# Depthwise taps as diagonal matmuls in 16 tiles of the array, the projection in row tiles, and one planner for all images

## The chip, the cores and the metric

One core of a Trainium2 chip runs the kernel in one launch. The metric is the device time of that launch in microseconds. Before the change the median of three runs is 9529.6 us (9521.79 to 9544.45).

## The reference, cut to what matters

The input is x, 64 images of 96 channels of 56x56 pixels in float32. Each image passes three parts, one after the other; C is 96, the middle width is 192, `bn` is a batch norm with fixed numbers.

```
out = silu(bn(expand_w @ x))                     # 1x1, 96 -> 192
out = channel_shuffle(shift_groups(out), 4)      # four groups moved by one pixel
dw  = bn(depthwise3x3(out)); idb = bn(out * id_w)
out = silu(bn(dw + idb))
se  = sigmoid(W2 @ relu(W1 @ mean_pixels(out)))  # grouped, 192 -> 24 -> 192
t   = silu(bn(proj_w @ (out * se)) + x)          # 192 -> 96
t   = t + bn(w2 @ real(ifft(relu(fft(relu(bn(w1 @ layernorm(t)))) * (r + i) + b))))
t   = t + ffn_fp8(layernorm(t))                  # 96 -> 384 -> 96, quantised
```

The Fourier transform runs over the 3136 pixels of an image for each of 192 channels.

## The kernel before, in words

Channels lie on partitions. The 96 channels of x and t stand in 112 partitions with a gap of 16 in the middle (`CP`, `GAP`), and one partition of the gap carries ones or a shift row. x has a border of one pixel (58x58), so that a shift is a window into it. x and t have two buffers each, by the image's parity (L104, L105); `load_x` (L112) fills an x buffer with two DMAs on SyncE's queue.

[...] the pool `psa` holds two tiles of two banks for the mixing, `psb` four tiles of one bank for all else.

An image goes through these functions, each a generator that yields after a step, so that steps of several images can be interleaved:

- `expand_a` (7 steps) and `expand_b` (5 steps): matmuls of 32 output columns, four side by side in the array (L297, L312), then a silu on ScalarE into `e_a` (128 channels, 58x58) or `e_b` (64 channels, the image's two halves stacked to 128 partitions, 30x58).
- `depthwise` (L329): three calls of nine steps, for the upper and lower half of `e_a` and for `e_b`. Each step is one VectorE instruction over 128x1568 elements (L341 for the first tap, L343 for the other eight), accumulating in `d_buf`. `mid_silu` (L346) applies bias and silu and sums the pixels, in three ScalarE instructions an image (L352).
- `excitation` (L357): the two small layers on the pixel sums, tanh in place of sigmoid, and the projection weights scaled by the gate (`pw`).
- `project` (L385): eight steps of seven rows, each three matmuls of 392 columns into one bank: an identity that brings x in (L395), the first 128 channels (L396) and the other 64 (L397). A silu writes t transposed (L400). After the last step it issues `load_x(b + 2)`.
- `deviations` (L406): the layer norm's factors. Per 448 columns one matmul centres t (L417), ScalarE squares (L419), four matmuls with one column take the mean (L426), VectorE adds epsilon (L427) and GpSimd raises to the power -0.5 (L428). `spread` puts the factors where the mixing needs them (L434, L441).
- `mixing` (L458): the Fourier part, in six stages that I call by the names of their plan: W1 (L468), F1 (L490), F2 (L518, L524, with ScalarE and VectorE steps L539 to L543 and `mirrored`), W2 (L555, L567), I1 (L590) and I2 (L608, added to t at L618).
- `ffn` (L628): 20 steps of layer norm and transposition (L639, L650, L656, L665), then 52 steps of the two fp8 layers (L674, L676, L684, L690, L692) and the store (L700, L702).

The order of all engines' work is written by a planner in the program (`merge`, L736). `PLAN` gives each stage of the mixing a length and each other function a first and a last due time, in the planner's own units counted from the start of one image's mixing. `merge` runs `mixing(b)` and after each of its steps all steps of the others that are due and whose needs are met; what is left is run when the mixing has ended, so nothing crosses from one image's mixing into the next. Beside `mixing(b)` run `ffn(b - 1)`, the last tap block, excitation, projection and deviations of image b + 1, and expand and the first two tap blocks of image b + 2. Images 0 and 1 are begun before the first mixing, one function after another. [...]

## Time and profile before

| what | value |
|---|---|
| median of three runs | 9529.6 us |
| the profiled execution, own time | 9484.53 us |
| its span | 9482.8 us |
| mean granted TensorE clock | 0.898 of full speed |
| instructions | 263604 |
| HBM read, written | 82.62 MB, 77.07 MB |
| one image's period in the middle (first W1 matmul to the next, median) | 146.7 us |
| first W1 matmul of image 0 | 172.7 us |
| end of the last image's mixing to the end of the span | about 51 us |

A row of the page's groups gives the source line, engine, operation and tiles, the shapes, the count, busy time in us, the mean of one in ns, and how long the engine was idle just before such instructions, with what ended that wait. An f32 matmul leaves two records, so counts of PE are twice the matmuls where the type is f32. Records of PE overlap: the time between two starts says more than the length of one. "PEclk" or "granted clock" is the share of full speed that the throttle gave TensorE.

### The profile page before, as it was taken

How to read it: one execution, taken by the hardware profiler on the slowest of the kernel's cores; microseconds unless marked ns; L12 is line 12 of the kernel's file. 1: busy time of each engine (PE TensorE's matmuls, PEld its weight loads, DVE VectorE, ACT ScalarE, POOL GpSimd, SP SyncE). 2: the span in 40 equal slices, each digit the busy share in tenths (PEclk: the TensorE clock that was granted, in tenths of full speed). 3: DMA queues.
4: the chain of work that ended last, by engine and by line, in shares of the span. 5: the costliest groups of instructions: out<-in, count | busy, mean ns of one | idle time of the engine just before them, and what ended most of it. 6: DMA issues, size and time to landing. Idle time of an engine off the chain costs nothing.

```text
span 9482.8 us, 263604 instructions
## 1 busy us (share of the span) xinstructions
PE 8133.7 (86%) x118530; PEld 6030.7 (64%) x118530; DVE 6389.5 (67%) x9034; ACT 4790.4 (51%) x9099; POOL 2240.6 (24%) x1360
## 2 busy tenths in 40 slices
PE   5888888888888888888888888888888888888887
PEld 3666666666666666666666666666666666666666
DVE  6667666666666766676666766666666666676764
ACT  2455454454554545545545545455455454554545
POOL 0222222222222222222222222222222222222221
PEclk8988999898888999999989989889998898888988
DMA  2111111111101111111111111111110111111100
GB/s 40 17 22 16 19 21 16 20 17 17 22 15 19 17 19 21 17 18 21 17 17 22 16 19 18 17 21 17 17 22 14 20 17 17 22 16 19 18 13 15
DMA packets 411399, 177.45 MB, mean 19 GB/s; under 512 B 366323, under 2 KB 409707, under 8 KB 410011
## 3 DMA queue, kind: packets, MB, share of 16 engines
q1 hardware_dynamic: 408508, 155.59, 13.0%
q8 instruction: 930, 15.24, 0.7%
q10 hardware_dynamic: 1264, 3.48, 0.1%
q0 software_dynamic: 496, 1.50, 0.1%
q14 instruction: 201, 1.64, 0.1%
HBM read 82.62 MB, written 77.07 MB: 17 GB/s over the span
## 4 chain that ended last, share of the span: by engine, by line
PE 67%; DVE 13%; ACT 9%; issue 6%; POOL 5%; DMA 0%; POOLq 0%; ACTq 0%; DVEq 0%
PE ps_f L490 8%; PE ps_i L608 7%; PE ps_c L417 5%; PE ps_i L590 5%; POOL rs L650 5%; PE ps_v L426 4%; PE ps_w L468 4%; PE ps_pj L395 4%; PE ps_w L555 4%; PE ps_pj L396 4%; PE ps_pj L397 3%; DVE d L343 3%; PE ps_f L524 3%; ACT h L684 3%; DVE buf_h L475 3%
## 5 line engine op out<-in xcount | busy, mean ns | idle before, releaser
L343 DVE SCALAR_TENSOR_TENSOR d<-e_a,taps,d 128x1568 f32<-128x1568 f32 x1024 | 1892.0, 1848 | 14.3
L428 POOL TENSOR_TENSOR rs<-v,mhalf 112x4 f32<-112x4 f32 x448 | 1060.1, 2373 | 2650.7 <-DVE v L427 2589.6
L700 POOL TENSOR_TENSOR o<-t,o 112x448 f32<-112x448 f32 x448 | 587.6, 1312 | 2921.7 <-DVE o L698 2921.7
L650 POOL TENSOR_TENSOR rs<-v,mhalf 112x4 f32<-112x4 f32 x448 | 582.8, 1301 | 1637.1 <-DVE v L649 1637.1
L343 DVE SCALAR_TENSOR_TENSOR d<-e_b,taps,d 128x1568 f32<-128x1568 f32 x512 | 943.4, 1843 | 0.5
L427 DVE TENSOR_SCALAR v<-ps_v 112x4 f32<-112x4 f32 x448 | 72.0, 161 | 1281.0 <-PE ps_v L426 1270.3
L490 PEld LDWEIGHTS ps_f<-f_tab,buf_h 128*64 128x64 f32 x24576 | 747.3, 138 | 163.5 <-DVE buf_h L475 57.2
L490 PE MATMUL ps_f<-f_tab,buf_h 128*64 128x58 f32 x24576 | 797.8, 223 | 40.0 <-DVE buf_h L475 40.0
L676 ACT CAST y<-ps_h 128x448 f16<-128x448 f32 x1344 | 723.9, 539 | 148.8 <-PE ps_h L674 130.2
L684 ACT CAST h<-y 128x448 fp8e5<-128x448 f16 x1344 | 770.4, 573 | 0.3 <-DVE y L681 0.3
L681 DVE TENSOR_SCALAR y<-y,qb 128x448 f16<-128x448 f16 x1344 | 649.1, 487 | 154.6 <-ACT y L676 135.4
L590 PE MATMUL ps_i<-inv_tab,buf_g 112*32 112x56 f32 x24576 | 482.4, 253 | 285.7 <-issue 284.8
L468 PE MATMUL ps_w<-w1c,t 112*64 112x96 f32 x14336 | 708.0, 250 | 0.0
L468 PEld LDWEIGHTS ps_w<-w1c,t 112*64 112x64 f32 x14336 | 611.6, 137 | 139.3 <-issue 117.0
L426 PEld LDWEIGHTS ps_v<-mean_m,sq 96*112 96x112 f32 x3584 | 516.2, 213 | 281.4 <-issue 257.2
L608 PE MATMUL ps_i<-r_tab,buf_h 64*64 64x56 f32 x14336 | 676.1, 276 | 1.0 <-ACT buf_h L597 1.0
L590 PEld LDWEIGHTS ps_i<-inv_tab,buf_g 112*32 112x32 f32 x24576 | 439.1, 139 | 339.8 <-issue 293.0
L608 PEld LDWEIGHTS ps_i<-r_tab,buf_h 64*64 64x64 f32 x14336 | 647.9, 189 | 5.0 <-ACT buf_h L597 1.1
L475 DVE SCALAR_TENSOR_TENSOR buf_h<-ps_w,rs_full 128x768 f32<-128x768 f32 (+1 forms) x512 | 437.3, 854 | 254.8 <-PE ps_w L468 245.8
L690 PE MATMUL ps_o<-h,q 128*112 128x448 fp8e5 x1344 | 421.3, 393 | 213.1 <-ACT h L684 213.0
L597 ACT COPY buf_h<-ps_i 128x896 f32<-128x896 f32 x192 | 174.0, 906 | 787.8 <-PE ps_i L590 787.8
L417 PE MATMUL ps_c<-t,center 112*96 112x448 f32 x896 | 553.2, 706 | 11.6 <-issue 10.9
(159 smaller groups left out, 14740.5 us busy)
## 6 DMA issues: line engine op xcount, KB each, us to landing
x<-in_x SPq DMA_DIRECT2D x128, 588.0 KB, 8.3
out_dram<-o SPq DMA_DIRECT2D x896, 84.0 KB, 1.9
l_tab<-in_tab_l ACTq DMA_DIRECT2D x1, 1624.0 KB
r_tab<-in_tab_r ACTq DMA_DIRECT2D x1, 1568.0 KB
t<-dev_t SPq DMA_DIRECT2D x64, 7.0 KB, 1.8
t<-dev_t SPq DMA_DIRECT2D x64, 5.2 KB
ex_row_p<-in_expand_row POOLq DMA_DIRECT2D x1, 336.0 KB, 4.2
s_p<-in_bn POOLq DMA_DIRECT2D x1, 288.0 KB, 4.0
```

The costliest lines, as they stand in the source:

```text
L343: nc.vector.scalar_tensor_tensor(dst, win, w, dst, ALU.mult, ALU.add)
L417: nc.tensor.matmul(cen, lhsT=center, rhs=t[:, g * 4 * CP : (g + 1) * 4 * CP], start=True, stop=True)
L426: nc.tensor.matmul(var[:, k : k + 1], lhsT=sq[:, k, :], rhs=mean_m, start=True, stop=True)
L428: nc.gpsimd.tensor_tensor(rs[:, js], v[:, js], mhalf[0:CP, 0:4], ALU.pow)
L468: nc.tensor.matmul(ps[hc * 64 : hc * 64 + 64, k, 0:C], lhsT=t[:, n0 : n0 + 64], rhs=w1c[:, hc * C : hc * C + C], start=True, stop=True,)
L475: nc.vector.scalar_tensor_tensor(h_v[:, :, d * NJ + j0 : d * NJ + j0 + n], ps[:, 0:n, 0:C].rearrange("p b c -> p c b"), 0.0, rs_full[:, d, ...
L490: nc.tensor.matmul(ps[r * 64 : r * 64 + 64, k, 0 : 2 * NK], lhsT=buf_h[:, n0 : n0 + 64], rhs=f_tab[:, r, :], start=True, stop=True,)
L590: nc.tensor.matmul(ps[p0 : p0 + 32, k, 0:HW], lhsT=u_v[:, oh * 48 + o, :], rhs=inv_tab[:, r, :], start=True, stop=True,)
L608: nc.tensor.matmul(ps[pr, bk, k, 0:HW], lhsT=buf_h[pr, n2 * 48 : n2 * 48 + 64], rhs=r_tab[pr, n2, :], start=True, stop=True,)
L650: nc.gpsimd.tensor_tensor(rs, v, mhalf[0:CP, 0:4], ALU.pow)
L676: nc.scalar.copy(y16, ps)
L684: nc.scalar.copy(held[i // 3][:, i % 3, :], held.pop(("y", i)), saturate=False)
```

## The change

- The nine taps become matmuls on TensorE. At the start a table `diag` is made of 32x32 diagonal blocks, one for each tap and each group of 32 channels. A depthwise call takes all four tiles of `psb`; for each tap it issues 16 matmuls of 7x56 columns, from four groups of channels (row tiles of the array) into four places of seven rows (column tiles). So a PSUM tile holds one channel group with its 28 rows spread over the partitions. Four ScalarE instructions then add the bias, apply silu and sum. `mid_silu` is gone. `d_buf` has the new layout, half, group, seven rows.
- Excitation follows that layout: 12 matmuls for the first layer, 24 for the second, one add and one tanh; the 0.5 of the sigmoid is folded into the projection weights.
- `project` works in two halves. Each issues 24 matmuls with 32 contraction rows in four row tiles, into four banks, and VectorE adds x in PSUM before the silu; the identity matmul is gone.
- `deviations` centres with four matmuls of 96 columns for each 448 pixels, as `ffn` does, and VectorE sums the squares, in place of the matmuls of one column.
- x has one buffer; `project(b)` ends with `load_x(b + 1)`.
- In `ffn` the second layer and the result come a step later.
- `merge` is replaced by `schedule`: every function of every image has a due time on one axis (image b is shifted by b times 116 units) and needs that reach across images, so a step can run beside any image's mixing. "hold" keeps all other planned functions out until the same function's next step, "part" keeps those that take all four banks out. The due times are new.

The core of the diff:

```
+NG = MID // 32
...
-    "mixing": (22.3, 18.0, 30.7, 18.0, 12.0, 23.2),
-    "ffn": (0.0, 63.5),
-    "expand_a": (1.2, 20.0),
-    "depthwise_2": (8.4, 36.3),
-    "silu_2": (37.3, 38.6),
-    "excitation": (42.0, 44.0),
-    "expand_b": (51.7, 59.7),
-    "project": (60.0, 86.0),
-    "depthwise_0": (80.6, 95.9),
-    "silu_0": (114.5, 118.3),
-    "depthwise_1": (96.1, 115.9),
-    "deviations": (87.0, 110.4),
-    "silu_1": (115.9, 118.2),
+    "mixing": (18.0, 18.0, 30.0, 18.0, 12.0, 20.0),
+    "ffn": (120.1, 178.7),
+    "expand_a": (-108.4, -87.5),
+    "expand_b": (-138.3, -112.4),
+    "depthwise_0": (-98.8, -98.7),
+    "depthwise_1": (-97.0, -92.0),
+    "depthwise_2": (-78.0, -74.3),
+    "excitation": (-74.6, -59.1),
+    "project": (-60.0, -40.0),
+    "deviations": (-60.8, -16.8),
...
-    x_buf = [const.tile([CP, PAD, PAD], F32, name=f"x_{i}") for i in range(2)]
+    xi = const.tile([CP, PAD, PAD], F32, name="x")
     t_buf = [const.tile([CP, NPIX + 8], F32, name=f"t_{i}") for i in range(2)]
-    for i in range(2):
-        nc.vector.memset(x_buf[i], 0.0)
-        nc.sync.dma_start(out=x_buf[i][GAP : GAP + 1].rearrange("p a b -> p (a b)"), in_=tab_ones)
+    nc.vector.memset(xi, 0.0)
+    nc.sync.dma_start(out=xi[GAP : GAP + 1].rearrange("p a b -> p (a b)"), in_=tab_ones)
...
+    eyes = load(tab_eyes, [128, 32], "eyes")
+    diag = const.tile([128, 2, 9, 32], F32, name="diag")
+    for h in range(2):
+        nc.vector.tensor_tensor(
+            diag[:, h],
+            eyes.unsqueeze(1).to_broadcast([128, 9, 32]),
+            taps[:, h, :].unsqueeze(2).to_broadcast([128, 9, 32]),
+            ALU.mult,
+        )
...
+    nc.vector.tensor_scalar(s[:, 0], s[:, 0], 0.5, None, ALU.mult)
+    for g in range(NG):
+        nc.vector.tensor_tensor(pj_w[:, g, :], pj_w[:, g, :], s[:, 0], ALU.mult)
...
-    d_buf = const.tile([128, 3 * HH, HW], F32, name="d")
-    def depthwise(b, i):
+    d_buf = const.tile([128, 2, NG, PJ, HW], F32, name="d")
+    def depthwise(b, i, cvs):
         if b >= NB:
             return
...
+        if b not in cvs:
+            cvs[b] = small.tile([128, 2, NG], F32, tag="sums", name="sums")
+        sums = cvs[b]
+        e, h, base = ((e_a, 0, 0), (e_a, 0, HH), (e_b, 1, 0))[i]
+        pss = [psb.tile([128, PJ, HW], F32, tag="psb", name="ps_d") for _ in range(4)]
+        for tap in range(9):
             dy, dx = divmod(tap, 3)
...
+            for j in range(4):
+                r0 = base + j * PJ + dy
+                for r in range(4):
+                    pr = slice(r * 32, r * 32 + 32)
+                    nc.tensor.matmul(
+                        pss[r][j * 32 : j * 32 + 32],
+                        lhsT=diag[pr, h, tap, :],
+                        rhs=e[pr, r0 : r0 + PJ, dx : dx + HW],
+                        start=tap == 0,
+                        stop=tap == 8,
+                    )
+            if tap % 3 == 2:
+                yield "hold"
+        for r in range(4):
+            s, g = (i, r) if i < 2 else (r // 2, 4 + r % 2)
+            nc.scalar.activation(
+                d_buf[:, s, g], pss[r], AF.Silu, bias=mid_b[:, g : g + 1], accum_out=sums[:, s, g : g + 1]
+            )
         yield
     def excitation(b, cvs):
             return
         sums = cvs[b]
         ps = psb.tile([128, 8], F32, tag="psb", name="ps_se")
-        for i in range(3):
+        for i in range(2 * NG):
+            s, g = divmod(i, NG)
             nc.tensor.matmul(
-                ps[0:24, 0:1], lhsT=rd_w[:, i // 2, :], rhs=sums[:, i : i + 1], start=i == 0, stop=i == 2
+                ps[0:24, 0:1], lhsT=rd_w[:, g, :], rhs=sums[:, s, g : g + 1], start=i == 0, stop=i == 2 * NG - 1
             )
...
+        ps = psb.tile([128, NG], F32, tag="psb", name="ps_se2")
+        gate = small.tile([128, NG], F32, tag="gate", name="gate")
+        for g in range(NG):
+            for j in range(4):
+                nc.tensor.matmul(ps[j * 32 : j * 32 + 32, g : g + 1], lhsT=ep_w[:, g, :], rhs=red, start=True, stop=True)
+        nc.vector.tensor_tensor(gate, ps, ep_b, ALU.add)
         yield
...
+        nc.scalar.activation(gate, gate, AF.Tanh, scale=0.5)
         yield
...
+        pw = small.tile([128, NG, CP], F32, tag="pw", name="pw", bufs=1)
+        nc.vector.scalar_tensor_tensor(
+            pw, gate.unsqueeze(2).to_broadcast([128, NG, CP]), 1.0, pj_w, ALU.add, ALU.mult
+        )
         cvs[b] = pw
         yield
     def project(b, cvs):
         if b >= NB:
             return
         pw = cvs.pop(b)
-        xi = x_buf[b % 2]
         tv = t_buf[b % 2][:, 0:NPIX].rearrange("p (b a) -> p b a", a=HW)
...
+        for s in range(2):
+            pss = [psb.tile([CP, PJ, HW], F32, tag="psb", name="ps_pj") for _ in range(4)]
+            for g in range(NG):
+                for j in range(4):
+                    pr = slice(j * 32, j * 32 + 32)
+                    nc.tensor.matmul(
+                        pss[j], lhsT=pw[pr, g, :], rhs=d_buf[pr, s, g], start=g == 0, stop=g == NG - 1
+                    )
+                if g == 2:
+                    yield "hold"
+            yield "hold"
+            for j in range(5):
+                if j < 4:
+                    r0 = s * HH + j * PJ
+                    nc.vector.tensor_tensor(
+                        pss[j], pss[j], xi[:, r0 + 1 : r0 + 1 + PJ, 1 : HW + 1], ALU.add
+                    )
+                if j:
+                    r0 = s * HH + (j - 1) * PJ
+                    nc.scalar.activation(
+                        tv[:, :, r0 : r0 + PJ], pss[j - 1].rearrange("p a b -> p b a"), AF.Silu, bias=pj_sh
+                    )
+                yield None if j == 4 else "hold"
+        load_x(b + 1)
...
...
+            cen = psb.tile([CP, 4, 128], F32, tag="psb", name="ps_c")
+            for k in range(4):
+                n0 = (g * 4 + k) * CP
+                nc.tensor.matmul(cen[:, k, 0:C], lhsT=t[:, n0 : n0 + CP], rhs=center, start=True, stop=True)
+            sqs[g] = work.tile([CP, 4, C], F32, tag="sq2", name="sq")
+            nc.scalar.activation(sqs[g], cen[:, :, 0:C], AF.Square)
         def variances(g):
-            sq = sqs.pop(g)
             js = slice(g * 4, g * 4 + 4)
...
+            nc.vector.tensor_reduce(v[:, js], sqs.pop(g), AX.X, ALU.add)
+            nc.vector.tensor_scalar(v[:, js], v[:, js], 1.0 / C, 1e-5, ALU.mult, ALU.add)
             nc.gpsimd.tensor_tensor(rs[:, js], v[:, js], mhalf[0:CP, 0:4], ALU.pow)
...
-            if m == 0:
-                held[j] = work.tile([128, 3, CH], F8, tag="h8", name="h8")
...
         def quantise(i):
+            if i % 3 == 0:
+                held[i // 3] = work.tile([128, 3, CH], F8, tag="h8", name="h8")
             nc.scalar.copy(held[i // 3][:, i % 3, :], held.pop(("y", i)), saturate=False)
...
-            yield
+            yield "part" if g <= ng else None
             if 2 <= g < ng + 2:
                 turn(g - 2)
-            yield
+            yield "part" if g <= ng else None
         n = 3 * NCH
-        for i in range(n + 5):
+        for i in range(n + 7):
             if i < n:
                 first(i)
             if 1 <= i <= n:
             yield
             if 2 <= i <= n + 1:
                 quantise(i - 2)
-            j, m = divmod(i - 5, 3)
-            if i >= 5 and m == 0 and j < NCH:
+            j, m = divmod(i - 6, 3)
+            if i >= 6 and m == 0 and j < NCH:
                 second(j)
-            if i >= 6 and m == 1 and j < NCH:
+            if i >= 6 and m == 2 and j < NCH:
...
+    SIDES = {
+        "ffn": (76, (("mixing", 0, None),)),
+        "expand_a": (7, (("project", 1, None),)),
+        "expand_b": (5, (("project", 1, None),)),
+        "depthwise_0": (4, (("expand_a", 0, 4),)),
+        "depthwise_1": (4, (("expand_a", 0, None),)),
+        "depthwise_2": (4, (("expand_b", 0, None),)),
+        "excitation": (4, (("depthwise_0", 0, None), ("depthwise_1", 0, None), ("depthwise_2", 0, None))),
+        "project": (14, (("excitation", 0, None), ("ffn", 2, None))),
+        "deviations": (10, (("project", 0, None), ("mixing", 1, 8))),
+    }
+    HOLD = ("depthwise_0", "depthwise_1", "depthwise_2", "project")
+    def schedule():
...
+        def one(until):
+            ready = [
+                (when, key)
+                for key, when in due.items()
+                if when < until
+                and (holder == [key] or not holder and not (part and key[0] in HOLD))
+                and met(SIDES[key[0]][1], key[1])
+            ]
+            if not ready:
+                return False
+            when, key = min(ready)
+            lo, hi = PLAN[key[0]]
+            step = next(sides[key], "end")
+            holder[:] = [key] if step == "hold" else []
+            part.discard(key)
+            if step == "part":
+                part.add(key)
+            if step == "end":
+                ended.add(key)
+                del due[key]
+            else:
+                done[key] = done.get(key, 0) + 1
+                due[key] = when + (hi - lo) / SIDES[key[0]][0]
+            return True
+        for b in range(NB):
+            while one(at):
+                pass
+            while ("deviations", b) not in ended:
+                one(1e9)
+            for w in mixing(b):
+                at += w
+                done["mixing", b] = done.get(("mixing", b), 0) + 1
+                while one(at):
+                    pass
+            ended.add(("mixing", b))
+        while one(1e9):
+            pass
...
```

## The prediction

> **What bounds the kernel now.** I read the page's engine shares, then the chain of waits, then the stretches of one image, then PE's own timeline. The shares say TensorE (PE) is the fullest engine and DVE second:
>
> ```profile
> PE 8133.7 (86%) x118530; PEld 6030.7 (64%) x118530; DVE 6389.5 (67%) x9034; ACT 4790.4 (51%) x9099; POOL 2240.6 (24%) x1360
> PE 67%; DVE 13%; ACT 9%; issue 6%; POOL 5%; DMA 0%; POOLq 0%; ACTq 0%; DVEq 0%
> L343 DVE SCALAR_TENSOR_TENSOR d<-e_a,taps,d 128x1568 f32<-128x1568 f32 x1024 | 1892.0, 1848 | 14.3
> L428 POOL TENSOR_TENSOR rs<-v,mhalf 112x4 f32<-112x4 f32 x448 | 1060.1, 2373 | 2650.7 <-DVE v L427 2589.6 <-DVE dev L432 59.4
> ```
>
> The reader should see that the taps (L343) are the biggest DVE item, but DVE is only 13% of the chain: the change moves work from the second engine to the first. Image after image repeats every 146.6 us. Cutting one such period where each mixing stage's first matmul starts (W1, F1, F2, W2, I1, I2) gives the table I work from. Columns: window, length, busy us and instructions of PE, PE weight load, DVE, ACT, POOL; granted PE clock, DMA share, GB/s.
>
> ```profile
> 4656.00:4686.70 30.70, 26.64 (x369) 18.57 (x367) 22.55 (x38) 13.92 (x27) 9.18 (x7) 1.00 0.00 1
> 4686.70:4704.40 17.70, 16.59 (x404) 13.45 (x404) 14.82 (x18) 14.84 (x32) 2.61 (x2) 1.00 0.09 24
> 4704.40:4740.60 36.20, 31.12 (x253) 19.63 (x254) 23.44 (x47) 29.64 (x57) 6.57 (x5) 0.95 0.09 25
> 4740.60:4759.40 18.80, 18.80 (x147) 13.66 (x147) 13.48 (x13) 7.39 (x12) 0.00 (x0) 1.00 0.18 20
> 4759.40:4783.40 24.00, 18.53 (x437) 14.69 (x436) 8.60 (x9) 5.95 (x9) 9.65 (x4) 0.72 0.51 38
> 4783.40:4802.60 19.20, 15.57 (x255) 14.24 (x254) 16.40 (x18) 2.98 (x7) 7.19 (x3) 0.65 0.01 2
> sum 146.60, PE 127.25 PEld 94.23 DVE 99.29 ACT 74.73 POOL 35.20; mean PE 21.21 PEld 15.71 DVE 16.55 ACT 12.45 POOL 5.87
> ```
>
> PE is idle 146.6 - 127.25 = 19.4 us per image. The last two rows show a second loss: the granted clock is 0.72 and 0.65. In us at full clock that is 24.0 x 0.28 + 19.2 x 0.35 + 36.2 x 0.05 = 15.2 us. So the period is about 112 us of PE work at full clock, 19 idle, 15 clock. What starts the slow clock is in PE's timeline of I1:
>
> ```profile
> 4763.43 0.86 PE L426 MATMUL ps_v<-mean_m,sq 96*112 96x1 f32 x8
> 4764.21 1.47 PE L590 MATMUL ps_i<-inv_tab,buf_g 112*32 112x56 f32 x101
> 4771.16 0.96 PE L590 MATMUL ps_i<-inv_tab,buf_g 112*32 112x56 f32 x27 [5.47 <-issue]
> 4772.05 1.81 PE L417 MATMUL ps_c<-t,center 112*96 112x448 f32 x2
> ```
>
> PE stops 5.47 us for nothing the profile names, inside a run of equal matmuls; afterwards ps_c takes 1.81 us instead of 0.97. In 4 us windows DMA moves 98 to 105 GB/s from 4756 to 4768, which is load_x (issued 4755.5); my reading is that PE's instructions queue behind it.
>
> [...] The trace has four column tiles only: 8 matmuls of L312 (16 records) start to next start in 1.46 us, where one untiled 392-column f32 matmul takes 0.66 (L395, start to start), so 8 x 0.66 / 1.46 = 3.6 times. [...] the same 112x4 pow takes 2373 ns at L428, beside taps, and 1301 at L650.
>
> **The change, part by part** (PE us per image at full clock).
> - Taps to PE: DVE loses 2835 us of L343 (both shapes) and 198 of L341, so 3033 / 64 = 47 us per image. PE gains 3 x 144 f32 matmuls of 392 columns. If all 16 tiles run together, a tap costs one 0.66: 3 x (9 x 0.66 + 0.4) = 19.0. Bounds: 17.8 (no tail)[...]. I take 19.0, since four tiles got 3.6 here.
> - Projection: out go 24 matmuls x 0.66 = 15.8. In come 48 of K=32 in four row tiles, 12 rounds x 0.66 = 7.9; I take 8.5 (bounds 7.9 and, at no gain, 15.8). The identity matmul becomes 8 DVE adds of 392 from PSUM, about 0.62 each as L618: 5 us of DVE. Four of them are queued ahead of F2's last pair of DVE steps, whose result W2's last group needs only 6 us later, so I cost that wait at nothing; without W2's first three groups it would be 2.5.
> - Squares: ps_c goes from 7 x 0.83 to four small matmuls like ps_n (8 records, 0.95): +0.9. ps_v goes, 7 x 0.69 = -4.8; in its place 7 DVE reductions of 0.54 (L648's row).
> - Excitation: 10 PE records become 72. L363 has 6 in 0.31 us, so 72 cost some 3.7, less 0.9 before: +2.5 (bounds 1 and 8, if they cost L372's 0.15 each).
> - Sum: 112 + 19.0 - 7.3 + 0.9 - 4.8 + 2.5 = 122.3. **PE work grows by 10 us per image.** ACT: three silus of 1.61 + 0.20 become twelve of about 0.55 + 0.20, +3.5 us; the squares' ACT work is as before.
> - One x buffer: load_x(b+1) is issued after project(b) instead of a period earlier. Two DMAs on SP's queue, behind the last projection add; dev_t rows and out_dram stores queue behind them briefly. It needs about 12 us. Until expand_b (first user) PE has W2's last group 1.8, six ps_c steps 5.7, I1 5.2 and one more ps_c, 13.7 us: hidden, by a little. Without that cover expand_b would wait up to 12.
> - Depthwise and projection take all four psb banks. Behind a finished block the next psb user waits for its first silu, some 1 us, five times; mixing's matmuls (psa) cover some of it. While PE runs a block of 6.3 us, ACT has nothing but its backlog.
> - The planner: working the due times through for a middle image puts expand_a and depthwise_0 in W1, depthwise_1 in F1, depthwise_2, excitation and half the projection in F2, the other half and six of the squares in W2, expand_b in I1 and I2. The first part of ffn stays in W1.
>
> **By stage** (before, then after). W1 30.7: PE 10.5 (W1 itself) + 8.7 (ps_n, ps_x) + 0.3 + 1.4 (expand_b's end) + 3.6 (four expand_a) + 6.3 = 30.8, with idle 2.5 instead of 4.1, because pow no longer waits for taps: 33.3. F1 17.7: 12.1 + 3.4 (ffn) + 2.7 + 6.3 = 24.5, idle as now: 25.5. F2 36.2: PE 27 but ACT 13.7 (F2) + 16.9 (ffn) + 3 + 2 = 35.6, already 29.6 there now, so ACT sets it: 37.5. W2 18.8: 9.2 + 4.2 + 5.7, plus a bank wait: 20.3. I1 and I2 together 43.2: PE 5.2 + 7.1 + 5.9 (four expand_b) + 2 = 20.2; ps_v and the 3.2 us wait for dev (DVE behind taps) are gone; the fetch stall, later against I1 than now, I put at 3.5 (0 to 5.5), other idle 3, clock loss 6.3 (0 to 12; now 13.4): 33. The sum is 149.6, **+3.0 per image**. Over 63 periods +189. The opening gets shorter: the first W1 starts at 172.7 us now, behind 47 us of image 0's taps and 31 of image 1's on DVE; with PE doing 19 I take 45 off. 189 - 45 = +144 on the profiled 9484.5 (span 9482.8), so 9629; the median of the runs, 9529.6, is 45 above that execution, and I carry the difference: **9675**.
>
> **Rivals.** (1) *The clock comes back*, and the change is faster. If load_x no longer starves I1, and denser work in I1 and I2 keeps the clock up, these stages take 20.2 + 3 = 23.2 and the period 139.8: 63 x -6.8 - 45 gives 9057; with the stall kept and half the clock loss, 144.6 and 9360. It decides when I1 and I2 fall below 30 us. For it: ps_v, the dev wait and 47 us of DVE go, and they stand in these very stages. Against: load_x still falls right ahead of I1, and PE was busy and slow at once. (2) *Sixteen tiles overlap poorly*[...] For it: the trace has no 16-tile case, and bank waits add to it. Against: 3.6 of 4. (3) *It cancels*: I1 and I2 at 30, no difference.
>
> **Numbers.** Mine 0.45, (1) 0.32, (2) 0.18, (3) 0.05. All of mine and (2) lie on the slow side, so slower 0.63, faster 0.32, same 0.05, within 0.2%, about what a measurement can tell. Mine alone spans 9550 to 9880 (clock loss and stall). The range 9190 to 10,090 leaves out the lower third of (1) and the upper half of (2).
>
> **What would show it.** PE busy at full clock near 122 us a period; 144 tap matmuls in 5.9 to 6.4 us (over 8: rival 2); projection's 24 in about 4.2; F1 near 25; POOL's pow near 1.0 us. Wrong if the clock of I1 and I2 is above 0.85, if no "issue" gap stands in I1, or if PE waits for psb banks beyond 6 us per image.

## The result and the profile after

The changed kernel takes 9693.5 us (median of four runs, 9687.0 to 9705.0), beside 9525.7 us for the kernel before on the same chip. The ratio is 1.0175, with a 95% interval of 1.0156 to 1.0193. **The change makes the kernel 1.75% slower.** The profiled execution is the one of 9686.95 us, with a span of 9685.1 us; the mean granted clock rises from 0.898 to 0.966.

Read the page in the same order as before: engine shares, chain, then the groups that the change added. In a group's row the two numbers behind the bar are busy us and mean ns of one record (records overlap: the 36,864 of the first ps_d row, 497 ns each, make 1098.0 us).

```profile
PE 8671.6 (90%) x179970; PEld 6371.6 (66%) x179970; DVE 3865.7 (40%) x8218; ACT 4814.9 (50%) x10190; POOL 1488.0 (15%) x1360
...
PE 69%; ACT 13%; DVE 12%; issue 4%; POOL 1%; DMA 0%; POOLq 0%; ACTq 0%; SPq 0%; DVEq 0%
...
L355 PE MATMUL ps_d<-e_a,diag 32*32 32x392 f32 x36864 | 1098.0, 497 | 28.1 <-ACT y L700 27.9
...
L412 PE MATMUL ps_pj<-d,pw 32*112 32x392 f32 x6144 | 740.2, 557 | 33.6 <-ACT t L426 28.4
...
L454 POOL TENSOR_TENSOR rs<-v,mhalf 112x4 f32<-112x4 f32 x448 | 442.3, 1010 | 1228.7 <-DVE v L453 1228.7
...
L355 PE MATMUL ps_d<-e_b,diag 32*32 32x392 f32 x18432 | 569.4, 497 | 13.5 <-ACT y L700 11.6
```

DVE has lost 2524 us and PE has gained 538, although PE now runs nearly always at full clock (0.966 on the mean). The taps are 1098.0 + 569.4 = 1667 us, 26.1 us per image; three blocks, so 8.7 us a block where I had said 6.3. The projection is 740.2 / 64 = 11.6 us per image, not 8.5. GpSimd's pow (L454) takes 1.01 us, as I said it would when no taps run beside it; beside taps it took 2.37 (L428 of the kernel before).

These are the stages W1, F1, F2, W2, I1, I2 of one image in the middle. The columns are those of the windows before: window, length, busy us and instructions of PE, PE weight load, DVE, ACT, POOL; then clock, DMA share, GB/s.

```profile
4788.60:4821.90 33.30, 30.81 (x644) 23.47 (x632) 15.84 (x31) 9.87 (x22) 7.05 (x7) 1.00 0.01 3
4821.90:4851.00 29.10, 27.71 (x715) 19.16 (x713) 3.77 (x10) 18.56 (x47) 1.14 (x1) 1.00 0.01 3
4851.00:4891.00 40.00, 32.91 (x552) 22.64 (x551) 23.83 (x50) 29.48 (x60) 7.37 (x7) 0.96 0.10 28
4891.00:4912.70 21.70, 21.68 (x227) 17.98 (x226) 11.99 (x30) 11.97 (x23) 6.46 (x7) 1.00 0.70 64
4912.70:4923.50 10.80, 7.36 (x408) 6.22 (x407) 0.78 (x3) 3.39 (x6) 1.07 (x2) 1.00 0.03 6
4923.50:4935.30 11.80, 11.80 (x290) 8.36 (x289) 3.66 (x7) 1.81 (x6) 0.00 (x0) 1.00 0.01 3
```

Look at the third number from the end of each row: the clock is 1.00 in I1 and I2, where it was 0.72 and 0.65, and the DMA share that stood in I1 (0.51) now stands in W2 (0.70), which was busy throughout all the same. (This image is one of the quicker ones: its I1 and I2 take 22.6 us, the median is in the table.) Medians over the images, us:

| stage | before | predicted | after |
|---|---|---|---|
| W1 | 30.7 | 33.3 | 33.2 |
| F1 | 17.6 | 25.5 | 29.2 |
| F2 | 36.2 | 37.5 | 40.1 |
| W2 | 18.8 | 20.3 | 21.7 |
| I1 and I2 | 43.3 | 33 | 24.0 |
| period, median | 146.7 | 149.6 | 149.0 |
| period, mean of 63 | 145.3 | | 149.3 |
| first W1 matmul | 172.7 | 127.7 | 124.2 |

The three parts of the time add up: the first W1 comes 48.5 us earlier, 63 periods are 4.04 us longer on the mean (+254), and what follows the last W1 is 3.5 us shorter: +202, the difference of the two spans (9685.1 - 9482.8).

So the change moved about 20 us per image each way. **Where it gained:** I1 and I2 lost 19.3 us. From the records of low clock, summed by stage and halved (at half speed, half the time is lost), the clock cost these two 11.7 us per image before and costs 1.4 now: -10.3. PE's idle time there, in the images shown, went from 9.1 to 3.4 us: -5.7. The remaining -3.2 is the balance of work: ps_v and most of ps_c left, and four steps of expand_b came. **Where it paid:** W1, F1, F2 and W2 gained 2.5, 11.6, 3.9 and 2.9 us.

The gaps of I1 and one block of taps, in PE's timeline (start, length, what, number of records, and in brackets the idle time ahead of it and what ended it):

```profile
4834.41 0.85 PE L355 MATMUL ps_d<-e_a,diag 32*32 32x392 f32 x6
4835.71 7.90 PE L355 MATMUL ps_d<-e_a,diag 32*32 32x392 f32 x282 [0.45 <-ACT y L700]
...
4912.80 2.36 PE L616 MATMUL ps_i<-inv_tab,buf_g 112*32 112x56 f32 x172
4916.90 1.78 PE L616 MATMUL ps_i<-inv_tab,buf_g 112*32 112x56 f32 x128 [1.75 <-issue]
4920.37 1.23 PE L616 MATMUL ps_i<-inv_tab,buf_g 112*32 112x56 f32 x82 [1.69 <-issue]
```

One gap of 5.47 us has become two of 1.75 and 1.69, each after well over a hundred records of the short ps_i matmuls, and the clock stays at 1.00 behind them in this image. (It doesn't in all: of 110 such stalls that began at full clock, 30 were followed by 0.5 within 3.5 us.) The block's records take 8.75 us. It starts with six records and then waits 0.45 us for a bank that ScalarE has yet to empty (the y at L700).

### The profile page after: what moved, and what is told of

Read it like the earlier page. It is cut to its first block, busy times and chain, and to the rows that moved or that the text cites. A ratio compares the mean times of both kernels' runs of the same rounds, so it can differ in the third digit from the quotient of the medians.

```text
span 9685.1 us, 387250 instructions
## 1 busy us (share of the span) xinstructions
PE 8671.6 (90%) x179970; PEld 6371.6 (66%) x179970; DVE 3865.7 (40%) x8218; ACT 4814.9 (50%) x10190; POOL 1488.0 (15%) x1360
## 4 chain that ended last, share of the span: by engine, by line
PE 69%; ACT 13%; DVE 12%; issue 4%; POOL 1%; DMA 0%; POOLq 0%; ACTq 0%; SPq 0%; DVEq 0%
PE ps_d L355 16%; PE ps_pj L412 7%; PE ps_f L516 7%; PE ps_w L494 6%; PE ps_i L634 5%; PE ps_eb L322 4%; PE ps_i L616 4%; PE ps_w L581 4%; PE ps_c L446 4%; PE ps_ea L308 3%; ACT y L700 3%; DVE s L566 3%; DVE ue L567 3%; ACT d L366 3%; ACT ue L565 3%
## 5 line engine op out<-in xcount | busy, mean ns | idle before, releaser
L355 PE MATMUL ps_d<-e_a,diag 32*32 32x392 f32 x36864 | 1098.0, 497 | 28.1 <-ACT y L700 27.9
L366 ACT ACTIVATE d<-ps_d,mid_b 128x392 f32<-128x392 f32 x768 | 440.9, 586 | 1248.4 <-PE ps_d L355 1248.4
L355 PEld LDWEIGHTS ps_d<-e_a,diag 32*32 32x32 f32 x36864 | 695.8, 103 | 361.0 <-ACT y L700 71.8
L676 POOL TENSOR_TENSOR rs<-v,mhalf 112x4 f32<-112x4 f32 x448 | 451.4, 1008 | 2518.8 <-DVE v L675 2518.8
L412 PE MATMUL ps_pj<-d,pw 32*112 32x392 f32 x6144 | 740.2, 557 | 33.6 <-ACT t L426 28.4
L544 PEld LDWEIGHTS ps_f<-l_tab,buf_g 128*128 128x128 f32 x3712 | 512.6, 219 | 344.5 <-PE ps_o L716 291.2
L700 ACT CAST y<-ps_h 128x448 f16<-128x448 f32 x1344 | 728.0, 542 | 8.4 <-PE ps_h L698 1.9
L698 PE MATMUL ps_h<-xq,q 96*128 96x448 fp8e5 x1344 | 470.8, 361 | 182.0 <-ACT d L366 84.4
L454 POOL TENSOR_TENSOR rs<-v,mhalf 112x4 f32<-112x4 f32 x448 | 442.3, 1010 | 1228.7 <-DVE v L453 1228.7
L412 PEld LDWEIGHTS ps_pj<-d,pw 32*112 32x112 f32 x6144 | 394.3, 195 | 312.0 <-ACT t L426 91.4
L544 PE MATMUL ps_f<-l_tab,buf_g 128*128 128x112 f32 x3712 | 548.9, 308 | 54.2 <-DVE ue L567 53.0
L355 PE MATMUL ps_d<-e_b,diag 32*32 32x392 f32 x18432 | 569.4, 497 | 13.5 <-ACT y L700 11.6
```

The lines of the kernel that those rows point to most:

```text
L355: nc.tensor.matmul(pss[r][j * 32 : j * 32 + 32], lhsT=diag[pr, h, tap, :], rhs=e[pr, r0 : r0 + PJ, dx : dx + HW], start=tap == 0, stop=tap ...
L366: nc.scalar.activation(d_buf[:, s, g], pss[r], AF.Silu, bias=mid_b[:, g : g + 1], accum_out=sums[:, s, g : g + 1])
L412: nc.tensor.matmul(pss[j], lhsT=pw[pr, g, :], rhs=d_buf[pr, s, g], start=g == 0, stop=g == NG - 1)
L544: nc.tensor.matmul(ps[:, k, 0:CP], lhsT=g_v[:, k1, 0:128], rhs=l_tab[:, k1, :], start=True, stop=True)
L700: nc.scalar.copy(y16, ps)
```

## The experiments

Two things were to be explained: why I1 and I2 became so short, and why the taps cost so much. My theory (in the expectations "A" mostly) was that load_x, two transfers of 588 KB each that run at once, holds up PE and starts the slow clock wherever it falls on the short matmuls of I1, and that the taps stand on PE's path at their full length. The rivals put I1's gain down to the column matmuls ps_v and the wait for dev, or to DVE's lighter load, and called the taps' length hidden.

**Leave out six of the nine taps** (after's kernel; only taps 0, 4 and 8 are computed).

```
-        for tap in range(9):
+        for tap in (0, 4, 8):
...
-            if tap % 3 == 2:
-                yield "hold"
+            yield "hold"
```

> The changed kernel with three of the nine taps (0, 4 and 8); six are left out, so this is not the same convolution. The taps keep PE busy 26.1 us per image after the change. Theory A (PE's own tap time lies on the path in W1, F1 and F2): two thirds of it go, 17.4 us per image, 64 x 17.4 = 1113, so 8580 to 8800 us. Rival B (what lengthens F1 and F2 is that a block holds all four banks and starves ACT, whatever its length): at most half of that, above 9100 us.

Measured: 8837.8 us, ratio to before 0.929 (0.927 to 0.931). The taps' records fall from 26.1 to 10.4 us per image, which takes 5.2 us from each block. The windows of W1, F1 and F2, one block in each:

```profile
4357.00:4385.10 28.10, 25.61 (x448) 19.48 (x436) 15.79 (x31) 9.85 (x22) 7.05 (x7) 1.00 0.01 2
4385.10:4409.10 24.00, 22.61 (x524) 15.32 (x521) 3.80 (x10) 18.59 (x47) 1.18 (x1) 1.00 0.01 3
4409.10:4446.30 37.20, 29.76 (x360) 19.78 (x359) 24.47 (x51) 29.30 (x60) 7.95 (x7) 0.86 0.11 30
```

W1 is shorter by 5.2 us and F1 by 5.1, the whole of a block's 5.2; F2 by 2.8, about half. So in W1 and F1 each us of taps is a us of the kernel, and in F2, where ScalarE is busy for 29.3 us, part of it is hidden. The period fell by 13.3 us for 15.7 us of taps. The time is just above A's range, far from B's.

**Put the column matmuls back** (after's kernel with the deviations' squares and variances of before).

```
...
-            nc.vector.tensor_reduce(v[:, js], sqs.pop(g), AX.X, ALU.add)
-            nc.vector.tensor_scalar(v[:, js], v[:, js], 1.0 / C, 1e-5, ALU.mult, ALU.add)
+            var = psb.tile([CP, 4], F32, tag="psb", name="ps_v")
+            for k in range(4):
+                nc.tensor.matmul(var[:, k : k + 1], lhsT=sq[:, k, :], rhs=mean_m, start=True, stop=True)
+            nc.vector.tensor_scalar(v[:, js], var, 1e-5, None, ALU.add)
```

> The changed kernel with the layer norm's factors as before: one 448-column centring matmul and four one-column matmuls (ps_v) per step. Theory A (the one-column matmuls are what lets the clock fall in W2, I1 and I2): PE work +3.9 us per image and the clock of those stages back near 0.7, together 7 to 12 us per image, 10150 to 10450 us. Rival B (the long stall behind load_x sets the clock, ps_v only costs its own time): 3.9 us, 9900 to 9980 us, and the clock stays above 0.95.

Measured: 9956.3 us, ratio to before 1.047 (1.045 to 1.049), 263 us above the changed kernel. The median period is 4.5 us longer. I1 and I2 stay at 11.7 and 11.8 us with a clock of 1.00; W2 grows from 21.7 to 26.7. B is right: ps_v costs its own time on PE, where it stands, and has no part in the slow clock of I1.

**Take them out of the kernel before.** The same edit the other way round, in the kernel before.

> The kernel before with only the layer norm's factors as in the change (four centring matmuls, VectorE sums). Theory A: PE work -3.9 us per image and the clock of I1 and I2 (0.72 and 0.65) well up: 8900 to 9250 us. Rival B: the sums queue on VectorE behind taps of 1.85 us each, the clock stays low because the stall behind load_x starts it: 9350 to 9650 us.

Measured: 9202.9 us, ratio 0.967 (0.965 to 0.969). Its I1 and I2:

```profile
4634.98:4654.28 19.30, 12.53 (x426) 11.60 (x424) 12.20 (x16) 5.17 (x8) 10.71 (x5) 0.73 0.62 47
4654.28:4672.59 18.31, 12.70 (x244) 11.95 (x244) 16.23 (x19) 3.42 (x8) 6.86 (x3) 0.81 0.01 2
```

The time is in A's range, but the clock of I1 is still 0.73, as B had it: 19.3 us for 12.5 us of busy PE. Most of the gain of 310 us (9512.6 for the kernel before, run beside it) is work that left: PE's work at full clock fell by 4.65 us per image, 298 us. The slow stages stay slow, I2 less so in this image (0.81, it was 0.65); on the mean the slow clock of the two cost 9.8 us per image instead of 11.7.

**Cut load_x into seven pieces** (the kernel before; all else is left as it was). Each piece is two transfers of 84 KB; the pieces are due one after another from the end of W2 to the middle of I2.

```
+    "load": (88.0, 116.0),
...
-        if b + 2 < NB:
-            load_x(b + 2)
+    def load_steps(b):
+        for j in range(NCH):
...
+                nc.sync.dma_start(
+                    out=xi[p0 : p0 + 48, 1 + r0 : 1 + r0 + RPC, 1 : HW + 1],
+                    in_=x[b, c0 : c0 + 48, j * CH : (j + 1) * CH].rearrange("c (a b) -> c a b", b=HW),
+                )
+            yield
...
+                    "load": (load_steps(b + 3), 7, {"project": 8}),
```

> The kernel before with only load_x cut into seven pieces of eight rows that are issued over W2, I1 and I2 instead of all at once. Theory A (PE's instructions wait behind the 12 us of load_x): the 5.2 us gap in I1 goes and the clock of I1 rises from 0.72, 8 to 12 us per image: 8750 to 9050 us. Rival B (the gap has another cause): within 60 us of the kernel before, the gap still there.

Measured: **8814.5 us, ratio 0.927 (0.925 to 0.928)**. I1 and I2, then three lines of PE's timeline:

```profile
4435.10:4448.10 13.00, 13.00 (x434) 10.61 (x434) 8.38 (x9) 5.84 (x10) 8.65 (x4) 1.00 0.02 5
4448.10:4466.00 17.90, 14.27 (x257) 12.99 (x256) 15.57 (x19) 3.16 (x8) 7.71 (x4) 0.71 0.16 31
```

```profile
4440.09 1.78 PE L603 MATMUL ps_i<-inv_tab,buf_g 112*32 112x56 f32 x128
...
4459.47 0.53 PE L447 MATMUL ps_dev<-eye,dev 112*12 112x112 f32 x2 [3.20 <-DVE dev L445]
4460.90 5.29 PE L621 MATMUL ps_i<-r_tab,buf_h 64*64 64x56 f32 x112
```

I1 is 13.0 us instead of 24.0, PE is busy for all of it and the clock is 1.00. In the list of waits (us in total, times, longest), the kernel before and then this one, PE's "issue" wait on ps_i nearly goes:

```profile
PE ps_i L590 <- issue: 284.8, 55, 5.9
PE ps_i L603 <- issue: 7.6, 9, 1.7
```

A is right, and this is the largest single effect of the study: 698 us from one edit that takes no work away. But the pieces did not go out where they were due. In the trace three are issued at the end of F2, one in W2 and three in I2, and none lands during I1 (DMA share 0.02), where 833 of the 1176 KB landed before. What the run shows is a load that is kept away from I1; whether pieces beside I1 would do no harm, it doesn't show. What slow clock is left stands in I2; it costs 4.2 us per image. The wait of 3.20 us for dev isn't what starts it: in this image the clock fell at 4454.69, 1.6 us before that wait began, and in 33 of 62 such waits it stood at 0.5 already. What does start it isn't shown.

**Both edits at once** (pieces, and ps_v out, in the kernel before).

> The kernel before with both single edits of the last runs: load_x in seven pieces (alone it gave 8814) and the layer norm's factors as in the change (alone it gave 310 us). Theory A (they are separate losses): the gains add up, 8430 to 8600 us. Rival B (both gains are the same clock loss, and VectorE's sums make the wait for dev longer): 8650 to 8820 us.

Measured: **8758.3 us, ratio 0.921 (0.919 to 0.923)**, the fastest version here. The two gains, 310 and 698 us, don't add: 56 us more than the pieces alone, as B said. PE's busy time fell by another 219 us, but its wait for dev rose from 230 to 357 us in total: the time freed on PE is spent waiting for DVE, which is 76% busy with its taps still on it.

**Undo the move of load_x** (after's kernel; load_x is issued beside W2's last group instead of at the end of the projection).

```
+    "load": (-32.2, -32.1),
...
+    def load_next(b):
         load_x(b + 1)
+        yield
...
```

> The changed kernel with load_x issued later, beside the last group of W2, so that its 12 us fall on I1 and no longer on the rest of the projection, the squares and W2. Theory A (in the change load_x no longer starves PE only because of where it falls): a gap of 3 to 6 us in I1, then half clock; I1 and I2 together grow from 24 to 33 to 38 us: 10250 to 10600 us. Rival B (denser work in I1 and I2 keeps the clock up, wherever load_x falls): no gap over 2.5 us, under 9900 us.

Measured: 10211.5 us, ratio to before 1.074 (1.072 to 1.077). I1 and I2 (window view), then two rows of the list of waits: us in total, times, longest.

```profile
5177.10:5195.50 18.40, 10.48 (x408) 7.82 (x407) 0.82 (x3) 3.54 (x7) 1.11 (x2) 0.77 0.78 69
5195.50:5209.60 14.10, 14.10 (x289) 9.96 (x289) 3.60 (x7) 1.68 (x4) 0.00 (x0) 0.82 0.01 4
```

```profile
PE ps_i L620 <- issue: 466.9, 129, 8.6
PE ps_eb L323 <- DMA x<-in_x: 93.0, 50, 14.9
```

All of the load lands during I1 now, the DMA share there is 0.78, PE stops for up to 8.6 us at a time, and the clock of I1 and I2 is 0.77 and 0.82 in the kernel that had 1.00. I1 and I2 went from 24.0 to 32.5 us. This is A's mechanism, at a slightly smaller price than its range. About 90 us of the 518 are another matter: expand_b waits for x itself.

**Order of the sixteen tiles** (after's kernel; row tile outside, column tile inside).

```
-            for j in range(4):
-                r0 = base + j * PJ + dy
-                for r in range(4):
-                    pr = slice(r * 32, r * 32 + 32)
+            for r in range(4):
+                pr = slice(r * 32, r * 32 + 32)
+                for j in range(4):
+                    r0 = base + j * PJ + dy
```

> The changed kernel with the tap matmuls in another order: for each row tile its four column tiles, in place of for each column tile its four row tiles. A block of 288 records takes 8.7 us now, against 5.9 if the 16 tiles streamed without a gap. Theory A (weight loads into one row tile hold each other and its matmuls up, so neighbours in the same row tile are worse): 9.5 to 12 us a block, 9850 to 10300 us. Rival B (the pace doesn't depend on the order): 8.5 to 8.9 us a block, 9650 to 9740 us.

Measured: 9507.0 us, ratio to before 0.9995 (0.9985 to 1.0006): as fast as before, and 186 us faster than the changed kernel. A block in PE's timeline:

```profile
4742.85 0.91 PE L355 MATMUL ps_d<-e_a,diag 32*32 32x392 f32 x24
4744.15 7.49 PE L355 MATMUL ps_d<-e_a,diag 32*32 32x392 f32 x264 [0.39 <-ACT y L700]
```

Both theories missed. The pace is nearly unchanged (0.83 us a tap on the median, 0.84 in the changed kernel), as B said, yet the time fell. Compare with the block shown for the changed kernel: there 6 records ran ahead of the wait for a bank, here 24 do. A matmul leaves two records (36,864 of ps_d<-e_a for 64 x 288 matmuls). With the row tile inside, the fourth matmul of the block already goes into the fourth bank, so that only three can run before the last bank is free; with it outside, each bank takes four matmuls in turn, and twelve can run. First start to last start is 7.8 us on the median instead of 8.5.

**Eight tiles at a time** (after's kernel; two row tiles by four column tiles, all nine taps, then the other two row tiles).

```
-        for tap in range(9):
+        for step in range(18):
+            half, tap = divmod(step, 9)
...
-                for r in range(4):
+                for r in (2 * half, 2 * half + 1):
...
```

> The changed kernel with the taps in eight tiles at a time: first all nine taps of row tiles 0 and 1, then of 2 and 3. Each tap's 16 passes of eight tiles take 0.66 us if weights come in time. Theory A (the 0.84 us a tap with 16 tiles is the weight loads falling behind, so eight tiles lose nothing): 0.66 a round, 12 us a block, 10250 to 10400 us. Rival B (the loss is in each pass, whatever the number of tiles): 0.84 a round, over 15 us a block, 10800 us or more.

Measured: 10,028.7 us, ratio to before 1.056 (1.053 to 1.059).

```profile
4982.25 11.72 PE L356 MATMUL ps_d<-e_a,diag 32*32 32x392 f32 x288
```

Each matmul has two records, and I call the first records of a round one pass and the second ones another. In this run a pass of eight tiles starts 0.329 to 0.330 us after the one before: 0.658 us a round, the same as one untiled matmul of 392 columns (L395 of the kernel before, 0.66 from start to start). So eight tiles took no longer than one; sixteen take 0.841 us a round in the changed kernel, in passes of about 0.35 and 0.49. So A is right on the pace; its reason, the weight loads, this run doesn't test. The price of 335 us is less than A's, because halves have a merit of their own: PE doesn't wait for banks ahead of a block any more (its idle time before ps_d is 0.0 us in total, 41.6 in the changed kernel), and the silus of the first half run during the second (ScalarE waits for ps_d 384 times, twice a block, instead of 192).

Four more runs were to be faster still. None beats the 8758.3 us, and each shows a wait that took another's place.

**Pieces, with the dev product on GpSimd** instead of VectorE, so that it doesn't stand behind taps.

```
-            nc.vector.tensor_tensor(dev[:, js], v[:, js], rs[:, js], ALU.mult)
+            nc.gpsimd.tensor_tensor(dev[:, js], v[:, js], rs[:, js], ALU.mult)
```

> The kernel before with load_x in seven pieces, and the product that makes dev moved from VectorE to GpSimd, so that it no longer queues behind taps of 1.85 us. Theory A (PE's wait of 3.2 us for dev is what lowers the clock in I2, 0.71 there): I2 shrinks from 17.9 to some 13 us, 8480 to 8600 us. Rival B (GpSimd's own pow is late, held by VectorE): PE still waits over 2 us for dev, 8700 to 8830 us.

Measured: 9196.5 us, ratio to before 0.967 (0.965 to 0.970); the pieces alone gave 8814.5.

```profile
4656.00 0.56 PE L447 MATMUL ps_dev<-eye,dev 112*16 112x112 f32 x2 [3.07 <-POOL dev L445]
...
4670.08 2.83 PE L481 MATMUL ps_w<-w1c,t 112*64 112x96 f32 x32 [3.42 <-issue]
```

PE waits as long as before, now for GpSimd, as B said, though the time is in neither range; and a new "issue" stall of up to 3.6 us stands at the start of W1, in 56 of the images. DVE's timeline shows what it is, though the list of waits doesn't name it:

```profile
4663.29 5.62 DVE L344 SCALAR_TENSOR_TENSOR d<-e_a,taps,d 128x1568 f32<-128x1568 f32 x3
4668.82 1.15 DVE L631 SCALAR_TENSOR_TENSOR t<-ps_i,bn2c_b,t 112x392 f32<-112x392 f32 x2
```

The second of these adds ends at 4669.98, and PE goes on at 4670.08. In all 56 stalls PE starts 0.10 us after such an add has ended. W1 takes its PSUM tiles from the same pool as I2, whose result the add reads, and the adds stand behind three taps: the stall is a wait for DVE, and neither the load nor its pieces. Behind it W1 runs at half clock, which costs 4.3 us per image here and 0.2 with the pieces alone.

**Pieces, with later due times**: deviations end at 118 units instead of 110.4, excitation is spread from 40 to 52.

> The kernel before with load_x in seven pieces and two planned stretches drawn out: deviations due from 87 to 118 units in place of 110.4, excitation from 40 to 52 in place of 42 to 44. Theory A (PE's 3.2 us wait for dev and the clock after it, 0.71 in I2, come from the last deviations steps standing too close together): 4 to 7 us per image less than with the pieces alone, 8350 to 8560 us. Rival B (VectorE stays behind with its taps wherever the step stands): 8700 to 8830 us.

Measured: 9497.6 us, ratio 0.9987 (0.9976 to 0.9998), far above both ranges.

```profile
4820.93 1.84 DVE L344 SCALAR_TENSOR_TENSOR d<-e_a,taps,d 128x1568 f32<-128x1568 f32 x1
4822.69 0.16 DVE L445 TENSOR_TENSOR dev<-v,rs 112x12 f32<-112x12 f32 x1
4823.00 0.53 PE L447 MATMUL ps_dev<-eye,dev 112*12 112x112 f32 x2 [7.16 <-DVE dev L445]
```

The wait for dev has grown from 3.2 to 7.2 us: a later place in the order put dev, 0.16 us of work, behind more taps on DVE. The clock is back at 0.900 and I2 at 26.7 us.

**The same due times with ps_v out as well.**

> As the last, with the layer norm's factors as in the change too. Theory A (these gave little beside the pieces, 56 us, only because the wait for dev grew to 5.6 us per image): with the wait gone PE's 3.9 us show, 150 to 300 us under the last kernel. Rival B (VectorE is what is full in I2): no faster than the last kernel.

Measured: 9526.3 us, ratio 1.0011 (1.0001 to 1.0022). The wait for dev is 798 us in total, I2 28.9 us: both together give no more than the plan alone, as B said.

**The new order of tiles, with the squares spread over W2 and I1** (after's kernel; deviations due from -38 to -14 units instead of -60.8 to -16.8).

> The changed kernel with the tap order of the last but one batch and the squares of the layer norm spread over W2 and I1 (due from -38 to -14 units in place of -60.8 to -16.8). Theory A (the two gaps of 1.7 us in I1 come from nothing but small matmuls standing there, faster than their instructions arrive): the gaps shrink to under 1 us per image, 9280 to 9400 us. Rival B (they are the tail of load_x): the gaps stay, 9480 to 9540 us.

Measured: 9626.9 us, ratio to before 1.013 (1.011 to 1.016), 120 us slower than the new order alone.

```profile
4871.06 0.69 PE L616 MATMUL ps_i<-inv_tab,buf_g 112*32 112x56 f32 x36
4875.10 2.45 PE L616 MATMUL ps_i<-inv_tab,buf_g 112*32 112x56 f32 x92 [3.35 <-issue]
```

Neither theory had this time. W2 did get shorter (21.7 to 17.8 us), but I1 grew from 12.3 to 17.9, with gaps of 3.35 us and more, and of the 56 stalls in I1 that began at full clock 49 were followed by 0.5. The squares were what stood between load_x and I1; without them 392 of the load's 1176 KB land during I1 again (19 in the changed kernel). This is a second, unplanned showing of what the late load_x showed.

## Why the prediction was right, and where it wasn't

The side and the time are near what I predicted (9675 against 9693). Three steps held as they stood: what leaves DVE and the opening (127.7 us said, 124.2 measured), the pow at 1.0 us, and W1 (33.3 against 33.2). That the time is so near is luck, in two ways. The period came right as a sum of two errors of opposite sign: F1, F2 and W2 took 7.7 us more than I said, I1 and I2 took 9.0 less. Over 63 periods either alone would have put the time near 10,160 or 9110 us, outside the 9550 to 9880 of my own reading. And the profiled executions differ by 202 us, where I had said 144; the 45 us from the profiled execution to the median, which I carried over, were 6.5 this time.

My own signs say the same. The pow, the stall that stays in I1 and the bank waits came as said. But a block of 8.7 us is past the 8 that I had set for rival 2, F1 is not near 25, and the clock of I1 and I2 (1.00 in the image shown, 0.94 on the mean) is above the 0.85 at which I had called the reading wrong.

**The step "If all 16 tiles run together, a tap costs one 0.66" failed.** A round of sixteen is 0.841 us, so a block is 8.7 us busy rather than 6.3, and the taps 26.1 us per image rather than 19.0. I had carried the 3.6 of 4 from four tiles to sixteen. The measured ratio is 16 x 0.658 / 0.841 = 12.5, where I took 16. The eight-tile run shows that the loss is in the step from eight to sixteen (0.658 and 0.841 us a round). Rival 2 was right that sixteen tiles overlap poorly, though the trace of before, with no sixteen tiles in it, showed no price for that. What it did not decide is the sign, since the kernel was slower either way.

**The projection's 8.5 was too low.** It is 11.6 us: its 24 matmuls of a half take 5.8 us on the mean, not 4.2. It lies between my bounds, 7.9 and 15.8. The excitation was costed too high (3.7 said, about 1.3 measured on PE), ps_c slightly too (6.7 against 6.0). Together: 122.3 + 7.1 + 3.1 - 2.4 - 0.7 = 129.4 us of PE a period at full clock; the trace has 135.5 busy less 5.1 of slow clock, 130.4. The 112 that I started from was itself low: I took off slow clock that fell on an idle PE, which I had counted as idle already. Of the 15.3 us in that period 12.4 fell on a busy PE, so the work was 114.8; counted that way it is 130.9 after the change, 16.1 more, where I had said 10. Another sum in the prediction doesn't come out either: in rival 1, 139.8 with the stall of 3.5 and half of 6.3 is 146.4 and not 144.6, some 9475 us and not 9360.

**In I1 and I2, the clock was the wrong term.** I put PE's work at 20.2, the fetch stall at 3.5, other idle at 3 and the slow clock at 6.3 us. Measured are 19.2, 3.4, nothing else that counts, and 1.4. The stall had the right size and the wrong consequence: I expected half the slow clock to follow from it, but behind the two gaps of 1.7 us shown there was none, where there was behind the one of 5.47. The clock also fell behind 30 other stalls of this kernel's I1, of 1.7 to 2.6 us, and no run here measured the length from which a gap counts. That PE was busy and slow at once, which I put against rival 1, stands in these windows of the kernel before, behind the gap of 5.47 us: 0.50 from 4772 to 4780, with PE busy throughout:

```profile
4772.00:4776.00 4.00, 4.00 (x15) 2.60 (x13) 0.80 (x2) 1.45 (x2) 0.56 (x1) 0.50 0.02 4
4776.00:4780.00 4.00, 4.00 (x94) 3.55 (x96) 3.91 (x4) 0.54 (x1) 3.70 (x2) 0.50 0.00 0
```

"Against: load_x still falls right ahead of I1" was the other half of the error. Six of the ps_c steps and W2's last group stand between the two, and W2's third group (2.7 us), which my sum of the cover left out. So the transfer runs beside W2 (1157 of 1176 KB, DMA share 0.70), where PE has 227 records in 21.70 us (408 in 10.80 in I1) and was busy for 21.68.

**Rival 1's mechanism came true, and the kernel was slower all the same.** Its deciding point, I1 and I2 below 30 us, was reached with 24.0. It was no deciding point: it took the other stages for given at my values, which were 7.7 us too low. A criterion for a sum has to name the whole sum.

F2 was said to be set by ScalarE (37.5). It is 40.1, and leaving two thirds of its taps out shortens it by half of what they take, so ScalarE and PE share it. Waits of PE for psb banks add up to some 302 us, 4.7 per image, below the 6 that I had named.

Why the changed kernel is slower, then: DVE lost work that was 13% of the chain at most, while 26.1 us of taps went on PE, fully on its path in two of three stages. Much of what pays for that is not in the change's arithmetic. It is that load_x no longer falls on I1: putting it back there costs I1 and I2 8.5 of the 19.3 us they had gained, and keeping it out of I1 in the kernel before, in pieces, takes 12.4 us off these stages and 7.3% off the time, without moving anything to PE.

**What PE waits for in an "issue" stall.** The list of waits names no cause, but the DMA packets do. Both pages have a queue of kind "instruction" (packets, MB, share), before and after:

```profile
q8 instruction: 930, 15.24, 0.7%
q8 instruction: 1409, 23.09, 1.0%
```

PE has 118530 matmul records and as many weight loads before, 179970 of each after. That is 255 of its instructions for each packet of 16 KB in both kernels, so a packet is worth some 128 records, the run between the two gaps of I1 shown above. In the kernel before all 63 "issue" stalls of PE of at least 1.2 us end 1.2 to 2.0 us after such a packet has ended, and after the change all 122 do; of PE's other waits of that length 4 of 142 and 13 of 113 have a packet there. I read these stalls as PE waiting for its instructions, with the transfer holding them up: in the kernel before the packet starts 2.3 us after PE has stopped (median), at 4767.95 in the image shown, as load_x runs out; in the changed kernel it starts 0.7 us before PE stops. By the same reading a stall is left in I1 after the change: 172, 128 and 82 records of ps_i run there with little between them, and 128 take 1.78 us, while 2.6 us pass (median) from the start of a packet to PE's going on.

**What stays open.** Cutting the load and moving it weren't tried apart. What makes the clock fall in I2 of the kernel before, ahead of the wait for dev, isn't shown. Why sixteen tiles lose a quarter where eight lose nothing isn't settled; 32 weight loads of 103 ns mean (their row's mean in the changed kernel) in each tap are a candidate, not shown.

## What to carry to other kernels

When a stage has a low clock, look for the gap ahead of it, and for what the DMA engines moved just then, before moving work between engines: keeping one large load away from a run of short matmuls was worth 698 us here, four times what the whole change cost (168). When the list of waits gives no cause for a stall, compare its end with the packets of the instruction queue and with the other engines' last instruction before it. When work goes to the fullest engine, price its rounds from a run with as many tiles (here 0.658 us with eight, 0.841 with sixteen), and take its full length as the cost wherever that engine's stretch is already full (here 5.2 and 5.1 of 5.2 us a block in W1 and F1). When several stages change at once, check the stages one by one: a sum that comes out right can hide two errors larger than itself.

## What the runs showed of the hardware

All of these are counts and times from the records of the runs named, and hold for them.

- Clock behind stalls: in I1 of the changed kernel 30 of 110 stalls that began at full clock (1.7 to 2.6 us, median 2.15) were followed by 0.5 within 3.5 us, and 80 (median 1.69) weren't. In the image shown of the kernel before the clock fell during a gap of 5.47 us, and also 2.7 us before a wait of 3.20, with only 0.43 us of idle PE in the 3.4 us ahead of the fall.
- Stretches at half clock: the kernel before had 218 of them, of 3.41 us (71), 6.83 (62), 10.24 (15), 13.65 (45) and 17.07 (21), and four longer ones.
- Taps in tiles of 32x32: a pass of 392 columns took 0.329 us with eight tiles in the array (the eight-tile run), as with one untiled matmul of the kernel before (0.66 for two); with sixteen, in the changed kernel, two passes took 0.841 us instead of 0.658.
- Load and stops of PE: a load of 1.2 MB (two transfers of 588 KB) at 98 to 105 GB/s went with stops of PE of 5.2 us on the mean in the kernel before (63 stalls) and up to 8.6 us where all of it fell on I1 (the late load_x), in a run of matmuls as short as ps_i (128 records in 1.78 us). In pieces, the same bytes took 7.8% of the 16 DMA engines' time instead of 13.0% (the first queue's row, 155.6 MB in both).
- Packets of the instruction queue: one of 16 KB took 1.04 us by itself (median of the kernel before) and 1.78 beside load_x, and PE went on some 1.4 us after its end (median in both kernels, 63 and 122 stalls).
